# A rotated, quantised feed-forward stage on one core: three engines issue in a written order, and the butterflies run across two iterations

## The chip, the cores and the metric

The kernel runs on one core of a Trainium2 chip. A core has a matrix engine (TensorE, called PE in the profile, with its weight loads shown apart as PEld), a vector engine (VectorE, DVE), a scalar engine (ScalarE, ACT), a general engine (GpSimd, POOL) and a queue processor that issues transfers (SyncE, SP). Matrix products land in PSUM[...]. The metric is the time of one execution on the device in microseconds; it is given as the median of several runs, beside one execution that was profiled.

## The reference

The input is 128 sequences of 32 tokens with 512 features, 4096 rows in all. Three blocks follow each other, each with a layer norm in front and a residual add behind: a cross attention, a delta-rule attention with its own gated MLP, and a feed-forward block whose inputs are rotated by a Hadamard transform and rounded to 8 bits, with ternary weights. Only the last block concerns the change:

```python
def h_bitlinear(x, w):
    xq = act_quant(fwht(x))
    wq = weight_quant(w)
    return jnp.einsum('bsh,oh->bso', xq, wq)
gate = h_bitlinear(hidden_states, w_gate)
up = h_bitlinear(hidden_states, w_up)
return h_bitlinear(jax.nn.silu(gate) * up, w_down)
```

`fwht` is a Walsh-Hadamard transform over all features of a row (512 for gate and up, 2048 for down). `act_quant` takes the largest absolute value of a row, scales it to 127 and rounds.

## The kernel before, in words

The program is written in Python; each call becomes an instruction of one engine. A scheduler of the framework then orders the instructions of each engine by the place they have in the program and by its own estimate of when each can start, and it hands out buffers and adds the waits between engines. So the order in which an engine works need not be the order of the source.

The last block is the class `HadamardFfn`. Its loop in `run` (L1093) goes over 32 tiles of 128 rows, with work of several tiles in each pass, so that the engines overlap:

- Tile i+2 is turned: PE transposes its four 128-column blocks (`transposed`, L97), ACT copies them (L1016), PE multiplies each by a 128x128 Hadamard matrix (`rotated`, L917). The rest of the 512-point transform, the part across blocks, was done in the stage before. DVE takes the largest absolute value (L952), small DVE steps of one column make the scale `qs` from it (`scales`, L927, L929, L930), ACT multiplies by it and adds a large constant that rounds (`rounded`, L935, here called the lift), DVE subtracts the constant (L939), and SP issues a transfer that transposes the bf16 integers (L955).
- Tile i is multiplied by the gate and up weights in four pieces of 512 columns (`middle`, L1032). For each piece ACT computes Silu (L1036) and DVE the product (L1037). The result `m` has 2048 columns. DVE then does the part of the 2048-point transform that crosses blocks: `butterflies`, four rounds of an add and a subtract over half the tile each (L126, L127).
- Tile i-1's `m` is transposed on PE into four banks (L97) and copied by ACT (L1044), rotated into four banks (L917), reduced to the largest value by DVE (L1051, L1055), scaled, lifted by ACT (L935) and lowered by ACT (L937), and transposed by a transfer of SP (L1068).
- Tile i-3 is finished: 16 matmuls with the down weights (L1077), a scaling on ACT (L1082), an accumulating transfer on POOL that adds the residual (L1083), and the output transfer on SP (L1084).

All PSUM tiles of the stage come from one pool of eight banks. A tile of 128x512 f32 takes one bank, and a bank can be taken again when its reader is through. The last tile has a form of its own: its integers are transposed by PE, not by a transfer (L1066).

Two tiles go through the first bullet during the stage before (`first`). That stage, a gated MLP in f32, keeps PE full until the loop begins.

Of the kernel before, what the change touches and what calls it, by code (L numbers as in the profile page):

```python
# [897 lines left out]

class HadamardFfn:
# [7 lines left out]
    def __init__(self, g, x2, z2, mv2, had, ffn, out):  # L907
        self.g, self.tc, self.nc = g, g.tc, g.nc
        self.x2, self.z2, self.mv2, self.had, self.ffn, self.out = x2, z2, mv2, had, ffn, out
        self.right = dict(bufs=1, side="right", reuse_waits="tile")  # L910
        self.ready = {}

    def rotated(self, ps, xT, c0):

        pr = ps.tile([P, D], FP, name="ps")
        for c in range(DC):
            self.nc.tensor.matmul(  # L917
# [4 lines left out]
    def scales(self, st, mx, c):  # L922


        nc = self.nc
        m = st.tile([P, 1], FP, name="m")
        nc.vector.tensor_scalar(m, mx, c, Q_EPS, ALU.mult, ALU.max)  # L927
        qs = st.tile([P, 1], FP, name="qs")
        nc.vector.reciprocal(qs, m)  # L929
        nc.vector.tensor_scalar(qs, qs, c, 127.0, ALU.mult, ALU.mult)  # L930
        return m, qs

    def rounded(self, q, t, pr, qs, scalar):
        nc = self.nc
        nc.scalar.activation(t, pr, AF.Identity, bias=self.magic, scale=qs)  # L935
        if scalar:
            nc.scalar.activation(q, t, AF.Identity, bias=self.minus)  # L937
        else:
            nc.vector.tensor_scalar(q, t, MAGIC, None, ALU.subtract)  # L939

    def statistics(self, ns):

        nc, rstd = self.nc, self.rstd
        nc.scalar.activation(rstd[:, ns], self.mv2[:, ns, 1], AF.Sqrt, bias=self.g.ln_eps)
        nc.vector.reciprocal(rstd[:, ns], rstd[:, ns])
        nc.vector.tensor_scalar_mul(rstd[:, ns], rstd[:, ns], self.C1)

    def integers(self, i, pr, st, q, qT, t):

        nc = self.nc  # L950
        mx = st.tile([P, 1], FP, name="mx")
        nc.vector.tensor_reduce(mx, pr, AX.X, ALU.max, apply_absolute_value=True)  # L952
        m, qs = self.scales(st, mx, self.rstd[:, i : i + 1])
        self.rounded(q, t, pr, qs, False)
        nc.sync.dma_start_transpose(qT, q)  # L955
        f = st.tile([P, 2], FP, name="f")
        nc.vector.tensor_scalar_mul(f, self.both, m)
        self.ready[i] = qT, f

    def open(self, ctx):  # L960
# [14 lines left out]
        self.both = wp.tile([P, 2], FP, name="both")  # L975
        nc.vector.tensor_copy(self.both[:, 0:1], sg)
        nc.vector.tensor_copy(self.both[:, 1:2], su)
        self.rstd = wp.tile([P, NT // P], FP, name="rstd")

    def first(self, ps):  # L980
# [3 lines left out]
        for i in range(2):  # L984
# [4 lines left out]
            nc.scalar.copy(zT, self.g.transposed(ps, z, self.g.ident))  # L989
# [3 lines left out]
            self.integers(i, self.rotated(ps, zT, 0), wp, q, qT, z)  # L993
            yield 1

    def run(self):
        tc, nc, g, NG = self.tc, self.nc, self.g, self.NG
        wg, wu, rotated = self.wg, self.wu, self.rotated
# [4 lines left out]
        stack, (st, xp, wk1, wk, mp1, ps) = pools(  # L1003
            tc, ("d_st", 6), ("d_x", 4), ("d_wk1", 3), ("d_wk", 3), ("d_m1", 2), ("d_ps", 8, PSUM),
        )
        with mpool as mp, tc.tile_pool(name="d_w2", **self.right) as wp2, stack:
            wd = wp2.tile([P, IC, D], BF, name="wq2")
            z = {}
# [4 lines left out]

            def turned(i):
                zT = wk1.tile([P, DC, P], FP, name="zT")
                nc.scalar.copy(zT, g.transposed(ps, z.pop(i), g.ident))  # L1016
                return zT

            def integers(i, pr):
                q = wk1.tile([P, D], BF, name="q")  # L1020
                qT = wk1.tile([P, DC, P], BF, name="qT")
                self.integers(i, pr, st, q, qT, wk.tile([P, D], FP, name="t"))

            def middle(qT, f):

                m = mp.tile([P, IF], FP, name="m")
                for k in range(NG):
                    ks = slice(k * D, (k + 1) * D)
                    pg, pu = (ps.tile([P, D], FP, name="ps") for _ in range(2))
# [213 lines left out]
```

## Time and profile before

| what | value |
|---|---|
| median of 3 runs | 3041.19 us (3034.57 to 3048.02) |
| profiled execution, its own time | 3032.95 us |
| span from its first to its last instruction | 3031.2 us |
| PE busy over the span | 2896.5 us (96%) |
| DVE busy | 2002.5 us (66%) |
| ACT busy | 1055.8 us (35%) |
| first and last transposes of a zt tile (start of the loop's passes 0 and 29) | 2409.59 and 2941.02 us |
| last rotation of an m tile | 2990.13 us |

In a profile, a row of instructions has its start or its count, its busy time and what it wrote and read by the names of the program's tiles (`ps<-ident,m` is a transpose of m into a PSUM tile). Square brackets give how long the engine stood idle before the row, and which instruction ended that idle time. In the list of waits, the columns are the total in microseconds, how often, and the longest. A matmul's end is modelled and consecutive ones overlap, so the distance between starts is a better measure of PE than its busy time.

### The profile page before, as it was taken

To read this page: it belongs to the slowest core of one execution; us is meant where nothing else is said; L and a number is where in the kernel's file an instruction comes from. 1 tells how busy PE (TensorE), PEld (TensorE's weight loads), DVE (VectorE), ACT (ScalarE), POOL (GpSimd) and SP (SyncE) were. 2 spreads that over 40 slices of the span, in tenths; PEclk is the share of its full clock that TensorE was granted. 3 is DMA by queue.
4 is the path that set the end of the run, shared out by engine and by line. 5 is a ranking of instruction groups with operands and counts; after the bars stand their busy time and mean duration, and the time that the engine had idled before them with its cause. 6 is when DMAs were issued, how large, how long until landed. Compare 5 with 4: busy or idle time off the path is not lost.

```text
span 3031.2 us, 40875 instructions
## 1 busy us (share of the span) xinstructions
PE 2896.5 (96%) x14934; PEld 1647.3 (54%) x14934; DVE 2002.5 (66%) x3373; ACT 1055.8 (35%) x1779; POOL 659.2 (22%) x962
## 2 busy tenths in 40 slices
PE   8999999999999999599999999999999999999997
PEld 3444444443333333266766677676666766666664
DVE  2353444326699797368787877878522398888886
ACT  1111111205656666422111122111211256566564
POOL 1121212112686676221211110111100000000000
PEclk9999999999999999799999999999999999999999
DMA  9797998863554543742414132231411124443333
GB/s 327 265 312 268 330 310 305 289 223 93 170 149 124 175 136 109 209 139 62 132 58 126 53 123 77 79 100 42 132 49 46 65 56 77 77 78 78 75 73 62
DMA packets 342169, 428.47 MB, mean 141 GB/s; under 512 B 150225, under 2 KB 252753, under 8 KB 338513
## 3 DMA queue, kind: packets, MB, share of 16 engines
q1 hardware_dynamic: 305888, 325.93, 36.0%
q0 software_dynamic: 36080, 99.92, 10.9%
q8 instruction: 119, 1.95, 0.3%
q14 instruction: 82, 0.66, 0.1%
HBM read 288.36 MB, written 93.85 MB: 126 GB/s over the span
## 4 chain that ended last, share of the span: by engine, by line
PE 48%; DVE 10%; ACT 5%; issue 2%; DMA 1%; POOL 0%; SPq 0%; ACTq 0%; DVEq 0%; POOLq 0%
PE pm L823 9%; PE pm L826 9%; PE pm L834 9%; PE pp L520 5%; PE ps L797 4%; ACT t L935 2%; PE ps L917 2%; PE ps L1077 2%; ACT q L937 2%; PE ps L1032 2%; PE ps L764 2%; PE pg L455 2%; DVE mb L126 2%; PE ps L97 2%; DVE mx L1051 1%
## 5 line engine op out<-in xcount | busy, mean ns | idle before, releaser
L823 PE MATMUL pm<-hT,wg 128*128 128x256 f32 x1408 | 342.5, 386 | 0.2 <-ACT hT L812 0.2
L826 PE MATMUL pm<-hT,wu 128*128 128x256 f32 x1408 | 333.6, 380 | 0.0
L436 DVE TENSOR_TENSOR pr<-L,W 128x1984 f32<-128x1984 f32 (+30 forms) x248 | 313.0, 1262 | 23.7 <-DMA L<-ld 19.8
L442 DVE TENSOR_TENSOR W<-W,pr 128x1984 f32<-128x1984 f32 (+30 forms) x248 | 308.2, 1243 | 3.2
L834 PE MATMUL pm<-wd,mT 128*128 128x512 f32 x704 | 307.4, 592 | 0.0
L823 PEld LDWEIGHTS pm<-hT,wg 128*128 128x128 f32 x1408 | 262.4, 191 | 56.8 <-issue 16.2
L826 PEld LDWEIGHTS pm<-hT,wu 128*128 128x128 f32 x1408 | 267.8, 190 | 36.2
L834 PEld LDWEIGHTS pm<-wd,mT 128*128 128x128 f32 x704 | 132.5, 190 | 160.1 <-issue 159.9
L1032 PE MATMUL ps<-wq,qT 128*128 128x512 bf16 x960 | 218.7, 379 | 0.3
L828 ACT ACTIVATE sg<-pm 128x256 f32<-128x256 f32 x176 | 67.2, 382 | 345.9 <-PE pm L823 334.4
L829 DVE TENSOR_TENSOR mT<-pm,sg 128x256 f32<-128x256 f32 x176 | 73.7, 419 | 160.8 <-PE pm L826 146.1
L1083 POOL DMA_DIRECT2D xo<-x x31 | 26.3, 848 | 582.6 <-ACT xo L1082 526.2
L1032 PEld LDWEIGHTS <-qT 128*128 128x128 bf16 x960 | 93.7, 98 | 103.0 <-issue 4.6
L461 POOL TENSOR_TENSOR kk<-kk,cm 128x256 f32<-128x256 f32 x128 | 132.0, 1031 | 2.1
L458 POOL DMA_DIRECT2D ld<-kk x128 | 92.5, 722 | 151.6 <-ACT kk L457 144.5
L935 ACT ACTIVATE t<-ps,magic,qs 128x512 f32<-128x512 f32 x158 | 115.9, 777 | 19.5 <-DVE qs L930 19.3
L455 PE MATMUL pg<-kqm,kq 128*32 128x512 f32 x896 | 118.8, 601 | 3.5 <-DMA kqm<-kq 2.9
L917 PEld LDWEIGHTS ps<-hd,mT 128*128 128x128 f32 x1024 | 119.6, 192 | 4.3
L346 PE MATMUL ps<-hT,wq 128*128 128x512 f32 x256 | 114.4, 606 | 7.8 <-ACT hT L339 7.8
L1077 PE MATMUL ps<-wq,q2T 128*128 128x512 bf16 x512 | 120.6, 391 | 0.5 <-ACT t L935 0.3
L917 PE MATMUL ps<-hd,mT 128*128 128x128 f32 x1024 | 119.7, 275 | 0.0
L520 PE MATMUL pp<-hT,wk 128*128 128x512 f32 x256 | 117.6, 600 | 0.7 <-DVE acc L527 0.4
(224 smaller groups left out, 4939.9 us busy)
## 6 DMA issues: line engine op xcount, KB each, us to landing
kall<-in_ctxT_dram SPq DMA_DIRECT2D x32, 2056.0 KB
cx<-in_ctx_dram SPq DMA_DIRECT2D x32, 2048.0 KB
x<-xo POOLq DMA_DIRECT2D x64, 256.0 KB, 3.5
ld<-kk POOLq DMA_DIRECT2D x128, 128.0 KB, 2.6
pd<-kk POOLq DMA_DIRECT2D x128, 128.0 KB, 2.3
L<-ld SPq DMA_DIRECT2D x8, 2048.0 KB
pe<-pd SPq DMA_DIRECT2D x256, 64.0 KB
kqm<-kq SPq DMA_DIRECT2D x448, 32.0 KB
```

Source lines behind the costliest of these rows:

```text
L436: nc.vector.tensor_mul(pr[:, 0:n], bc(L[:, s, :, s + 1 : T].rearrange("p h t -> p t h"), HD), w[:, s].unsqueeze(1).to_broadcast([P, n, H4, ...
L442: nc.vector.tensor_sub(w[:, s + 1 :], w[:, s + 1 :], pr[:, 0:n])
L455: nc.tensor.matmul(pg[js], k[:, js], m[:, :, :, js], start=True, stop=True)
L461: nc.gpsimd.tensor_mul(kk[:, 1], kk[:, 1], cm.unsqueeze(1).to_broadcast([P, HH, T]))
L520: nc.tensor.matmul(pp.rearrange("p b t -> p (b t)"), w[n][:, dc, ec * P : (ec + 1) * P], hT[:, dc, :], start=dc == 0, stop=dc == DC - 1,)
L823: nc.tensor.matmul(pg, wg[:, dc, fs], hT[:, dc, :], start=dc == 0, stop=dc == DC - 1)
L826: nc.tensor.matmul(pu, wu[:, dc, fs], hT[:, dc, :], start=dc == 0, stop=dc == DC - 1)
L834: nc.tensor.matmul(pd, mT[:, fc, i * P : (i + 1) * P], wd[:, fc, :], start=fc == 0, stop=fc == FC - 1,)
L917: self.nc.tensor.matmul(pr[:, c * P : (c + 1) * P], xT[:, c0 + c, :], self.hd, start=True, stop=True)
L935: nc.scalar.activation(t, pr, AF.Identity, bias=self.magic, scale=qs)
L1032: nc.tensor.matmul(p, qT[:, dc, :], w[:, dc, ks], start=dc == 0, stop=dc == DC - 1)
L1077: nc.tensor.matmul(pd, qT[:, c, :], wd[:, c, :], start=c == 0, stop=c == IC - 1)
```

## The change

A new class `InOrder` wraps an engine; each instruction issued through it gets an edge to the previous one. The edge carries no semaphore; it only keeps the scheduler from exchanging the two. `run` wraps PE, ACT and DVE, and the loop is written anew so that the source has the order wanted on each of them. SP and POOL stay with the scheduler.

In a pass, the order is now as follows. PE: transposes of tile i+2, first gate/up piece, rotation of tile i+2, three gate/up pieces, transposes of m of tile i-1, down product of tile i-3, rotation of m of tile i-1. ACT: copy of tile i+2, first lift of tile i-2's second rounding, first Silu, three more lifts, two Silu, the first lowering, the fourth Silu, the lift of tile i+2, four copies of m, three lowerings, the scaling of tile i-3. DVE: the sixth butterfly of tile i-1, first product, the seventh and eighth, second product, the largest value and scales of tile i+2, third and fourth product, the lowering of tile i+2, four butterflies of tile i, the first reduction of tile i-1, the fifth butterfly of tile i, three reductions and the scale steps of tile i-1. The eight butterflies of a tile are a generator, of which five run in one pass and three in the next.

The second rounding of a tile thus begins in one pass and ends in the next, and its down product comes one pass after the integers instead of two. The transposed and the rotated z share a PSUM pool of one bank (`pz`); the other pool has seven. The lifts get a pool of six `t` tiles. The layer norm's factor of a row is moved out of the scale and into the constants `both` and `floor`, computed once for all tiles, so that `scales` has a multiplication and a reciprocal and no third step. After the loop the last two down products follow one after the other, the final tile being lowered by DVE alone.

```diff
+class InOrder:
+
+
+    def __init__(self, tc, engine):
+        self.tc, self.engine, self.last = tc, engine, None
+
+    def __getattr__(self, name):
+        method = getattr(self.engine, name)
+
+        def issue(*args, **kw):
+            ins = method(*args, **kw).ins
+            if self.last is not None:
+                self.tc.add_manual_dep(
+                    ins, self.last.name,
+                    mybir.DependencyInfo(
+                        mybir.DependencyClass.NoSync, mybir.DependencyReason.DATA
+                    ),
+                    reason="in order",
+                )
+            self.last = ins
+
+        return issue
...
-    def scales(self, st, mx, c):
-
-
-        nc = self.nc
+    def scales(self, st, mx, floor):
+
         m = st.tile([P, 1], FP, name="m")
-        nc.vector.tensor_scalar(m, mx, c, Q_EPS, ALU.mult, ALU.max)
+        self.dve.tensor_scalar(m, mx, floor, 1.0 / 127.0, ALU.max, ALU.mult)
         qs = st.tile([P, 1], FP, name="qs")
-        nc.vector.reciprocal(qs, m)
-        nc.vector.tensor_scalar(qs, qs, c, 127.0, ALU.mult, ALU.mult)
+        self.dve.reciprocal(qs, m)
         return m, qs
 
-    def rounded(self, q, t, pr, qs, scalar):
-        nc = self.nc
-        nc.scalar.activation(t, pr, AF.Identity, bias=self.magic, scale=qs)
-        if scalar:
-            nc.scalar.activation(q, t, AF.Identity, bias=self.minus)
-        else:
-            nc.vector.tensor_scalar(q, t, MAGIC, None, ALU.subtract)
+    def lifted(self, t, pr, qs):
+
+        self.act.activation(t, pr, AF.Identity, bias=self.magic, scale=qs)
...
+    def largest(self, i, pr, st):
+
         mx = st.tile([P, 1], FP, name="mx")
-        nc.vector.tensor_reduce(mx, pr, AX.X, ALU.max, apply_absolute_value=True)
-        m, qs = self.scales(st, mx, self.rstd[:, i : i + 1])
-        self.rounded(q, t, pr, qs, False)
-        nc.sync.dma_start_transpose(qT, q)
+        self.dve.tensor_reduce(mx, pr, AX.X, ALU.max, apply_absolute_value=True)
+        m, qs = self.scales(st, mx, self.floor[:, i : i + 1])
         f = st.tile([P, 2], FP, name="f")
-        nc.vector.tensor_scalar_mul(f, self.both, m)
+        self.dve.tensor_scalar_mul(f, self.both[:, i, :], m)
+        return qs, f
+
+    def integers(self, i, pr, f, qs, q, qT, t):
+
+        self.lifted(t, pr, qs)
+        self.dve.tensor_scalar(q, t, MAGIC, None, ALU.subtract)
+        self.nc.sync.dma_start_transpose(qT, q)
         self.ready[i] = qT, f
...
+            pr = self.rotated(ps, zT, 0)
+            qs, f = self.largest(i, pr, wp)
+            f0 = wp.tile([P, 2], FP, name=f"f{i}")
+            nc.vector.tensor_copy(f0, f)
+            self.integers(i, pr, f0, qs, q, qT, z)
             yield 1
...
+        pe, act, dve = (InOrder(tc, e) for e in (nc.tensor, nc.scalar, nc.vector))
+        self.pe, self.act, self.dve = pe, act, dve
...
-        stack, (st, xp, wk1, wk, mp1, ps) = pools(
-            tc, ("d_st", 6), ("d_x", 4), ("d_wk1", 3), ("d_wk", 3), ("d_m1", 2), ("d_ps", 8, PSUM),
+        stack, (st, xp, wk1, wk, tp, mp1, ps, pz) = pools(
+            tc, ("d_st", 6), ("d_x", 4), ("d_wk1", 3), ("d_wk", 3), ("d_t", 6), ("d_m1", 2),
+            ("d_ps", 7, PSUM), ("d_pz", 1, PSUM),
         )
...
+            def butterflies(i):
+
+                a, b = m[i], mp.tile([P, IF], FP, name="mb")
+                step = 1
+                while step < IC:
+                    x, y = (
+                        v.rearrange("p (a c d) -> p a c d", c=2, d=step * P) for v in (a, b)
+                    )
+                    dve.tensor_add(y[:, :, 0, :], x[:, :, 0, :], x[:, :, 1, :])
+                    yield
+                    dve.tensor_sub(y[:, :, 1, :], x[:, :, 0, :], x[:, :, 1, :])
+                    yield
+                    a, b, step = b, a, 2 * step
...
+            def last_rotated(mT, steps):
+
+
+                mx = st.tile([P, NG], FP, name="mx4")
+                pr = []
                 for k in range(NG):
-                    pt = g.transposed(ps, m[:, k * D : (k + 1) * D], g.ident)
-                    nc.scalar.copy(mT[:, k * DC : (k + 1) * DC, :], pt)
-                return mT
-
-            def last_integers(pr, end):
-
-                mx = st.tile([P, NG], FP, name="mx4")
-                for k in range(NG):
-                    nc.vector.tensor_reduce(
+                    pr.append(self.rotated(ps, mT, k * DC))
+                    dve.tensor_reduce(
                         mx[:, k : k + 1], pr[k], AX.X, ALU.max, apply_absolute_value=True
                     )
+                    if k == 0:
+                        go(steps, 1)
...
+                dve.tensor_reduce(mx1, mx, AX.X, ALU.max)
+                mm, qs = self.scales(st, mx1, Q_EPS / self.C2)
                 f = st.tile([P, 1], FP, name="fd")
-                nc.vector.tensor_mul(f, mm, sd)
-                return qT, f
+                dve.tensor_mul(f, mm, sdl)
+                return pr, qs, f
 
...
-            m, done = {}, {}
-            for i in range(n + 3):
-                if i + 2 < n:
-                    zT = turned(i + 2)
+            steps, last = iter(()), None
+            for i in range(n + 1):
+                cur, ahead = i < n, i + 2 < n
+                if ahead:
+                    zT = wk1.tile([P, DC, P], FP, name="zT")
+                    act.copy(zT, self.transposed(pz, z.pop(i + 2), g.ident))
                 if 0 < i and i + 5 < n:
                     load(i + 5)
-                if i < n:
-                    steps = middle(*self.ready.pop(i))
-                    m[i] = next(steps)
                 if i == n // 2:
                     self.statistics(slice(late, n))
-                if i + 2 < n:
-                    integers(i + 2, rotated(ps, zT, 0))
-                if i < n:
-                    for _ in steps:
-                        pass
-                if 0 <= i - 1 < n:
-                    mT = middle_turned(m.pop(i - 1))
-                if 0 <= i - 3:
-                    finish(i - 3, *done.pop(i - 3))
-                if i == n - 1:
-                    x_end = xp.tile([P, D], FP, name="zt")
-                    nc.sync.dma_start(x_end, self.x2[i * P :, :])
-                if 0 <= i - 1 < n:
-                    pr = [rotated(ps, mT, k * DC) for k in range(NG)]
-                    done[i - 1] = last_integers(pr, i == n)
-                if i < n:
-                    m[i] = butterflies(nc, m[i], mp.tile([P, IF], FP, name="mb"))
+                if cur:
+                    qT, f = self.ready.pop(i)
+                    m[i] = mp.tile([P, IF], FP, name="m")
+                    p = gate_up(qT, 0)
+                elif 0 <= i - 3:
+                    finish(i - 3, *qT2.pop(i - 3))
+                if last:
+                    pr2, qs2, f2 = last
+                    q2 = mp1.tile([P, IF], BF, name="q2")
+                    q2T = mp1.tile([P, IC, P], BF, name="q2T")
+                    t2 = [tp.tile([P, D], FP, name="t") for _ in range(NG)]
+
+                    def lowered(k):
+                        act.activation(
+                            q2[:, k * D : (k + 1) * D], t2[k], AF.Identity, bias=self.minus
+                        )
+
+                    self.lifted(t2[0], pr2[0], qs2)
+                go(steps, 1)
+                if cur:
+                    s = gated(p[0], f)
+                if last:
+                    for k in range(1, NG):
+                        self.lifted(t2[k], pr2[k], qs2)
+                if cur:
+                    times_up(m[i], 0, p[1], f, s)
+                go(steps, IC)
+                if ahead:
+                    pr = self.rotated(pz, zT, 0)
+                if cur:
+                    p = gate_up(qT, 1)
+                    times_up(m[i], 1, p[1], f, gated(p[0], f))
+                if ahead:
+                    qs, fn = self.largest(i + 2, pr, st)
+                if cur:
+                    p = gate_up(qT, 2)
+                    s = gated(p[0], f)
+                if last:
+                    lowered(0)
+                if cur:
+                    times_up(m[i], 2, p[1], f, s)
+                    p = gate_up(qT, 3)
+                    times_up(m[i], 3, p[1], f, gated(p[0], f))
+                if ahead:
+                    self.integers(
+                        i + 2, pr, fn, qs, wk1.tile([P, D], BF, name="q"),
+                        wk1.tile([P, DC, P], BF, name="qT"), tp.tile([P, D], FP, name="t"),
+                    )
+                if 0 <= i - 1:
+                    mT = turned(i - 1)
+                if last:
+                    for k in range(1, NG):
+                        lowered(k)
+                    nc.sync.dma_start_transpose(q2T, q2)
+                    qT2[i - 2] = q2T, f2
+                if cur and 0 <= i - 3:
+                    finish(i - 3, *qT2.pop(i - 3))
+                if cur:
+                    steps = butterflies(i)
+                    go(steps, NG)
+                if 0 <= i - 1:
+                    last = last_rotated(mT, steps)
+
+            x_end = xp.tile([P, D], FP, name="zt")
+            nc.sync.dma_start(x_end, self.x2[(n - 1) * P :, :])
+            finish(n - 2, *qT2.pop(n - 2))
+            pr, qs, f = last
+            q2T = mp1.tile([P, IC, P], BF, name="q2T")
+            q2 = mp1.tile([P, IF], BF, name="q2")
+            for k in range(NG):
+                t = tp.tile([P, D], FP, name="t")
+                self.lifted(t, pr[k], qs)
+                q = q2[:, k * D : (k + 1) * D]
+                dve.tensor_scalar(q, t, MAGIC, None, ALU.subtract)
+                copy = act.copy if k % 2 else dve.tensor_copy
+                copy(q2T[:, k * DC : (k + 1) * DC, :], self.transposed(ps, q, g.identb, BF))
+            finish(n - 1, q2T, f)
 
 
 @with_exitstack
```

## The prediction

> **What bounds the kernel now.** I read the page's first two parts, then the stretches, the waits and the timeline of the last stage.
>
> ```profile
> span 3031.2 us, 40875 instructions
> PE   8999999999999999599999999999999999999997
> PEclk9999999999999999799999999999999999999999
> ```
>
> ```profile
> 2650.00:2700.00 50.00, 47.49 (x294) 31.12 (x293) 42.47 (x71) 31.85 (x54) 2.54 (x3) 1.00 0.42 77
> ```
>
> The second block is a 50 us stretch of the stage that changes; its columns are PE, PEld, DVE, ACT and POOL busy (instructions in brackets), clock, DMA share, GB/s. The stage fills the last 620 us. PE is at 95% there, so it looks like the bound; but DVE (85%) is close, and a busy matmul row can hide a pause shorter than its modelled end. The pauses are clearer in the waits from 2472.9 to 2941, exactly 25 iterations:
>
> ```profile
> DVE q L939 <- ACT t L935: 50.5, 17, 3.0
> PEld ps L97 <- ACT t L935: 29.0, 49, 1.5
> ACT t L935 <- DVE qs L930: 13.7, 16, 1.1
> PEld ps L97 <- ACT s L1036: 5.5, 8, 0.7
> PEld ps L97 <- DVE m L1037: 3.6, 16, 0.3
> ```
>
> The weight loads of the transposes (L97) wait 29.0+5.5+3.6 = 38.1 us, 1.52 us an iteration, for a PSUM bank, mostly until ACT's first rounding step (L935) has read it. One iteration shows why the bank is late:
>
> ```profile
> 2658.37 2.48 DVE L1051 TENSOR_REDUCE mx<-ps 128x1 f32<-128x512 f32 x4
> 2659.89 0.60 PE L97 MATMUL ps<-ident,zt 128*128 128x128 f32 x4
> 2661.90 0.15 DVE L1055 TENSOR_REDUCE mx<-mx 128x1 f32<-128x4 f32 x1
> ...
> 2663.10 0.15 DVE L927 TENSOR_SCALAR m<-mx 128x1 f32<-128x1 f32 x1
> ...
> 2663.82 0.15 DVE L929 RECIPROCAL qs<-m 128x1 f32<-128x1 f32 x1
> ...
> 2665.08 0.15 DVE L930 TENSOR_SCALAR qs<-qs 128x1 f32<-128x1 f32 x1
> ...
> 2668.71 0.42 PEld L97 LDWEIGHTS ps<-ident,m 128*128 128x128 f32 x4 [0.92 <-ACT t L935]
> ...
> 2671.17 0.42 PEld L97 LDWEIGHTS ps<-ident,m 128*128 128x128 f32 x4 [0.69 <-ACT s L1036]
> ...
> 2671.84 3.61 PE L1077 MATMUL ps<-wq,q2T 128*128 128x512 bf16 x16
> ...
> 2675.29 3.73 PE L917 MATMUL ps<-hd,mT 128*128 128x128 f32 x32
> ```
>
> The reductions end at 2660.85; the scale that frees four banks is ready at 2665.23, because each 0.15 us step queues behind a 1.22 us butterfly. Starts of the zt transposes are 17.50, 18.98 and 19.42 us apart in rotation; over i=4 to 28 the mean is (2941.02−2472.95)/25 = 18.72.
>
> [...] two of the 25 iterations took 21.0 instead of 19.4, and their 50 us stretches show clock 0.97 against 1.00 above.
>
> **The change, part by part.** *PE floor.* PE executes the same instructions. Start to start in the timeline: zt transposes 0.43 (2659.89 to 2660.32), first gate/up half 1.73, rotation of z 0.89, 24 gate/up matmuls 5.2 (a row of 24 lasts 5.34, less its last one's overlap), 16 transposes of m 1.74 (0.109 each, the pitch in the row of four zt transposes), down 2671.84 to 2675.29 = 3.45, rotation of m 2675.29 to 2678.86 = 3.57. Sum 17.0; with hand-offs 17.1. That agrees with 18.63 (the three-step mean) less 1.52.
>
> *DVE, in the new order.* Pitches are start to start in the timeline. Eight butterflies at 1.14 (2663.95 to 2665.08), 9.12, plus 0.10 where the third reads the second (2674.33 to 2675.58 is 1.25); four gate products at 0.66, 2.64; five reductions at 0.60 (four last 2.48), 3.0; q 0.38. The small steps now follow each other directly, so each waits for the last: after the last reduction 0.12+0.19+0.19+0.08+0.12 = 0.70, as the tail already shows from 3010.38 to 3010.96; for z 0.12+0.25+0.08+0.11 = 0.56, as from 2413.73 to 2415.02. Sum 16.5. The two removed L930 would have cost about 0.2. The first gate product waits some 0.3 for ACT: 16.8. ACT: four Silu of 0.69, five lifts of 0.78, four lowerings of 0.72, copies 2.06+0.58, a scaling of 0.71: 12.9. PE remains the bound, with only 0.3 of cover on DVE.
>
> *The order laid side by side* (us after an iteration's start). The last rotation ends at 17.2 of the previous one, so its last scale is ready at about 1.7. ACT: zT 0.6, first lift 1.8 to 2.6, Silu to 3.2, three lifts to 5.2. DVE: sixth butterfly from 1.8, gate product 3.2, seventh and eighth to 6.2. PE needs m only at 8.3: cover 2.1. Lifts release banks at 2.6, 3.9, 4.5 and 5.2; taken in turn, PE wants them at 3.9, 4.8, 5.6 and 6.5: cover 1.1 to 1.4. Gate products end by 9.3, q 9.7, four butterflies 14.2; the first last-rotation bank is full at 14.6, so DVE is there first. If a cover is gone, the excess goes one to one on PE. I take 17.15 an iteration (17.0 to 17.5).
>
> *The bank for z, and eight minus one.* z's transposes and its rotation share a bank; its round trip ends when ACT lifts it at 8.9, before the next z at 17.1. Cost zero, behind 8 us; seven other banks are the cover counted above.
>
> *Transposing transfers.* SP still issues q2T, q's, the output and the z load. The down product follows q2T one iteration sooner: lowered by 12.9, wanted 10.1 into the next, 14.2 us later. No view gives that transfer's time. In the tail it starts issuing at 3006.03 and its user runs at 3016.30: at most 10.3; its packets end about 5 us after issue, so I take 5 (nothing exposed). An output queued on SP ahead would add about 6 and still fit.
>
> *Start.* Iteration 3 ended at 2472.95, 63.4 after 2409.59. In the new order DVE starts four butterflies at 9.4, then needs about 16.5 an iteration; PE waits for it in iterations 1 to 3 (banks not lifted) and ends iteration 3 at 62.1. Gain 1.3, bounds −4 and +5.
>
> *Middle.* i=4 to 31 took from 2472.95 to 2993.7 (last rotation's start 2990.13 + 3.57), 520.8. After: 28 x 17.15 = 480.2, less 2.7 for z's PE work absent from two = 477.5. Gain 43.3. This includes the two slow-clock iterations.
>
> *Tail.* From 2993.7 to the end, 37.5. PE no longer pauses 5.3 us for butterflies, but the last-but-one down product now stands ahead of the final transposes, and its ACT scaling ahead of the final lifts. Final rotation ends at 13; q2T of that tile, lowered at 12.7, is taken at about 18; the down product and scaling end at 22.5; four lift/lower/transpose/copy rounds of about 2 each end at 30.4; down to 33.4, final add and output to about 40. Loss 2.8, bounds −4 (a gain) and +6.
>
> *Once only.* Extra multiplies in the statistics, the f0 copies and moved scale constants are under ten small DVE operations; zero, beside the last mlp block's PE work. The second statistics call may put two ACT_TABLE_LOAD of 1.28 in mid-stage: at most 2.6, behind ACT's 4.2 spare.
>
> Sum 1.3+43.3−2.8 = 41.8: the profiled execution, 3032.95, becomes 2991.2. The runs' median is 8.2 above that execution; taking that offset along, 2999.
>
> **Rivals.** (A) As above: 2982 to 3012; floor 17.0, better ends and the spread of 13 us among the runs give the lower end. (B) DVE becomes the bound: 0.3 us of cover is little, and every wait in a fixed DVE order is paid. Before, DVE stood idle 2.4 us an iteration, but could fill in with ready work. For it: 16.8 against 17.1. Against it: those idles were mostly q behind ACT (50.5/25), which now follows an ACT queue that is early. At 17.9: 28x0.75 = 21 more, 3020. (C) The gain is not there: the same banks stay late (the lifts now wait for reductions at the iteration's boundary, ahead of Silu), and the start loses what the middle gains. At 18.6, 3040. Against it: the scale chain shrinks from 4.4 us after its reductions to about 1. (D) Slower: the down product, first of a strict queue, waits for q2T. It decides from 14.2+2 = 16.2 us after the last lowering, since 2 us an iteration (28x2 = 56) eats the gain; at 17 us, 2999+28x2.8 = 3077. For it: SP must wait for an accumulating write before each output. Against it: 5 us seen.
>
> **How the numbers follow.** A change of 0.5%, 15 us, is what can be told from none. Chances A 0.65, B 0.16, C 0.10, D 0.09; A and B are faster (0.81), C the same, D slower. The range holds A and B with the run spread: 2980 to 3028; the likeliest case alone is 2982 to 3012.
>
> **What would show it.** Right: zt starts 17.0 to 17.5 apart; no weight load of L97's successor waiting for a lift; the scale within 1.5 us of the last reduction; DVE near 95%; no 0.97 clock in the middle. B: PE waits on DVE's eighth butterfly or on lifts late for qs, DVE without idle time. C: zt starts above 18.4. D: PE idle ahead of the down product, ended by a DMA. Wrong would be a DVE sum off by 5%, banks assigned otherwise than in turn, or a tail longer than 46.

## The result and the profile after

The changed kernel takes 2992.93 us in the median of six runs (2982.3 to 2995.91), the kernel before 3035.48 (six runs, 3030.14 to 3048.02). The ratio is 0.985, with an interval of [0.983, 0.987]: 1.5% faster. The forecast was 2999, in a range of 2980 to 3028. The profiled execution of after took 2991.72 us; its span is 2989.9.

The stage of the change, cut at the same places in both traces (us). It begins with the first transposes of a zt tile; the middle runs from those of pass 4 to the end of the rotation of m in pass 31 (its start and 3.57); the tail is what follows:

| | before | after | after by the prediction |
|---|---|---|---|
| start, passes 0 to 3 | 63.36 | 62.57 | 62.1 |
| middle, passes 4 to 31 | 520.75 | 473.58 | 477.5 |
| tail | 37.48 | 38.80 | 40.3 |
| whole stage | 621.59 | 574.95 | 579.9 |
| all that lies before the stage | 2409.59 | 2414.99 | 2409.59 |

The stage gained 46.6 us, 4.8 more than predicted. In this profiled execution the work before the stage took 5.4 us longer, of which some 3.4 by an estimate (half of 6.8): stretches of half clock (granted 0.50) between 1227 and 1296 us, in another stage, add up to 47.8 us there and to 41.0 before. The rest was not traced to a cause. In the nine traces of the changed kernel and of kernels made from it, the stage begins between 2406.2 and 2417.8 us, so 5.4 us lies within the spread of executions. So the profiled execution's 2991.72 falls on the sum's 2991.2 by luck: 4.8 too little gain and 5.4 of something else.

From the page of after, its span, PE's tenths and the granted clock:

```profile
span 2989.9 us, 40853 instructions
...
PE   8999999999999999699999999999999999999997
...
PEclk9999999999999999799999999999999999999999
```

The tenths look as before, since 95% and 100% both print a 9. The stretch from 2650 to 2700 us shows the difference (columns: PE, PEld, DVE, ACT, POOL busy with counts, clock, DMA share, GB/s):

```profile
2650.00:2700.00 50.00, 50.00 (x321) 33.97 (x320) 48.03 (x73) 34.47 (x57) 2.54 (x3) 1.00 0.42 87
```

PE is busy throughout, with 321 matmul records where before had 294 in the same 50 us. DVE rose from 85% to 96%. The waits from 2472 to 2910 us follow; after issues everything of the loop through one helper, so all lines read L909 and the tiles tell what it is:

```profile
ACT t L909 <- DVE qs L909: 16.7, 28, 1.6
...
DVE m L909 <- ACT s L909: 6.1, 26, 0.2
DVE mx L909 <- PE ps L909: 5.0, 22, 0.2
```

No row of PE or PEld is left; before, weight loads for the transposes of m (L97) waited 38.1 us in passes 4 to 28. One pass, which begins at 2664.62 with the transposes of zt:

```profile
2663.88 1.88 DVE L909 TENSOR_REDUCE mx<-ps 128x1 f32<-128x512 f32 x3
2664.62 0.60 PE L909 MATMUL ps<-ident,zt 128*128 128x128 f32 x4
...
2665.79 0.16 DVE L909 TENSOR_REDUCE mx<-mx 128x1 f32<-128x4 f32 x1
...
2666.17 0.16 DVE L909 RECIPROCAL qs<-m 128x1 f32<-128x1 f32 x1
...
2666.37 0.78 ACT L909 ACTIVATE t<-ps,magic,qs 128x512 f32<-128x512 f32 x1 [0.53 <-DVE qs L909]
...
2667.62 2.12 ACT L909 ACTIVATE t<-ps,magic,qs 128x512 f32<-128x512 f32 x3
...
2672.78 0.77 ACT L909 ACTIVATE t<-ps,magic,qs 128x512 f32<-128x512 f32 x1
2672.85 1.91 PE L909 MATMUL ps<-ident,m 128*128 128x128 f32 x16
```

The scale stands within 0.6 us of the last reduction instead of 4.4, the lifts follow, and the 16 transposes of m form one row with no wait in it. The next zt transposes come 17.00 later; every pass from 2477.56 on takes 17.00 to 17.01.

### The profile page after: what moved, and what is told of

It reads as the page before. It is cut to its first block, busy times and chain, and to the rows that moved or that the text cites. A ratio compares the mean times of both kernels' runs of the same rounds, so it can differ in the third digit from the quotient of the medians.

```text
span 2989.9 us, 40853 instructions
## 1 busy us (share of the span) xinstructions
PE 2879.6 (96%) x14934; PEld 1649.2 (55%) x14934; DVE 2008.9 (67%) x3318; ACT 1057.1 (35%) x1777; POOL 659.4 (22%) x962
## 4 chain that ended last, share of the span: by engine, by line
PE 59%; DVE 5%; DMA 2%; issue 1%; ACT 1%; SPq 0%; POOL 0%; DVEq 0%; ACTq 0%; POOLq 0%
PE ps L909 17%; PE pm L823 9%; PE pm L834 9%; PE pm L826 9%; PE pp L520 5%; PE ps L797 4%; PE pg L455 2%; PE ps L764 2%; DVE W L442 1%; DVE pr L436 1%; DMA xs<-x 1%; PE ps L97 1%; DMA wd<-in_WdownT_dram 1%; DVE m L909 0%; PE pm L455 0%
## 5 line engine op out<-in xcount | busy, mean ns | idle before, releaser
L823 PEld LDWEIGHTS pm<-hT,wg 128*128 128x128 f32 x1408 | 262.1, 191 | 57.0 <-issue 16.2
L909 PE MATMUL ps<-wq,qT 128*128 128x512 bf16 x960 | 217.1, 379 | 3.0 <-ACT t L909 3.0
L909 DVE TENSOR_TENSOR mb<-m 128x1024 f32<-128x1024 f32 x128 | 153.1, 1217 | 0.1
L909 DVE TENSOR_TENSOR m<-mb 128x1024 f32<-128x1024 f32 x128 | 150.7, 1219 | 1.2
L909 PEld LDWEIGHTS <-qT 128*128 128x128 bf16 x960 | 93.9, 98 | 103.7 <-issue 3.9
L909 ACT ACTIVATE t<-ps,magic,qs 128x512 f32<-128x512 f32 x158 | 115.7, 781 | 37.7 <-DVE qs L909 37.7
L909 PEld LDWEIGHTS ps<-hd,mT 128*128 128x128 f32 x1024 | 120.7, 194 | 8.9 <-ACT mT L909 4.8
L909 PE MATMUL ps<-hd,mT 128*128 128x128 f32 x1024 | 121.4, 278 | 4.1 <-ACT mT L909 4.1
L909 PE MATMUL ps<-wq,q2T 128*128 128x512 bf16 x512 | 120.2, 389 | 3.8 <-DMA q2T<-q 3.8
```

What stands on the lines that cost most here:

```text
L823: nc.tensor.matmul(pg, wg[:, dc, fs], hT[:, dc, :], start=dc == 0, stop=dc == DC - 1)
L909: ins = method(*args, **kw).ins
```

## Experiments

Four questions: does the held order pay, what else does, how much cover has DVE, and what does the tail's order cost. In the tables and texts, "middle" and "tail" are cut as above.

### Is it the order?

**The chain off.** The changed source, without the edges, so that the scheduler may exchange neighbours.

```diff
-        pe, act, dve = (InOrder(tc, e) for e in (nc.tensor, nc.scalar, nc.vector))
+        pe, act, dve = nc.tensor, nc.scalar, nc.vector
```

> The changed kernel without the chain: the same source order, split butterflies and banks, but the scheduler may again exchange instructions of PE, ACT and DVE. My theory (what pays is that the order is held, above all the scale steps standing directly behind the last reduction): the steps fall between butterflies again, PE's transposes of m wait for banks, passes 18 to 19 us apart, 28 x 1.0 to 2.0 = 28 to 55 us lost, so 3020 to 3045. Rival (the new source order, the split and the shorter scale do it, and the chain changes little): passes 17.0 to 17.3, 2990 to 3003.

Measured: 2991.95 us, ratio 0.985 [0.983, 0.987], the same as the changed kernel. The passes take 17.03, later 17.21; the middle is 6.5 us longer than with the edges (480.06), the tail 3.3 shorter (35.46). The theory that the held order earns the gain fell: the edges are worth 0.23 us a pass, and in the sum nothing. Its timeline (L1121 and L960 are small steps of the scale, L1090 is a butterfly, L965 the lifts):

```profile
2684.76 0.15 DVE L1121 TENSOR_REDUCE mx<-mx 128x1 f32<-128x4 f32 x1
2684.87 1.23 DVE L1090 TENSOR_TENSOR m<-mb 128x1024 f32<-128x1024 f32 x1
...
2686.74 0.15 DVE L960 RECIPROCAL qs<-m 128x1 f32<-128x1 f32 x1
...
2686.92 2.78 ACT L965 ACTIVATE t<-ps,magic,qs 128x512 f32<-128x512 f32 x4 [0.23 <-DVE qs L960]
```

The small steps still stand between long DVE work, and the lifts come 5.0 us into the pass instead of 1.75, yet PE hardly waits. So the late scale, in which the prediction saw the reason for the late banks, can't be all of it.

**The butterflies unsplit.** All eight before the reductions of the same pass, with the edges; then the same source without them.

```diff
-                    go(steps, NG)
+                    go(steps, IC)
```

> The changed kernel with all eight butterflies of a tile ahead of the reductions of its own pass, none carried over. My theory: DVE's sum is the same 16.5 a pass, but the first product now directly follows the scale steps and waits for lift and Silu (about 0.1+0.66+0.69 = 1.45 us, which the sixth butterfly filled), and the scale comes some 4 us later in the pass, so passes of 17.6 to 18.2 with DVE as the bound: 28 x 0.6 to 1.2 = 17 to 34 more than 2993, so 3010 to 3027. Rival (the split is only cosmetic, since DVE has 4% idle time and PE leads): 17.0, 2993.

Measured: 3091.18 us, ratio 1.018 [1.016, 1.020]: slower than before. Most passes take 18.95 and 21.68 by turns, some 19.99 each; the mean is 20.24 where 17.6 to 18.2 was expected. One of the long ones, which began at 2889.05:

```profile
2892.04 2.47 DVE L909 TENSOR_REDUCE mx<-ps 128x1 f32<-128x512 f32 x4
...
2895.12 0.78 ACT L909 ACTIVATE t<-ps,magic,qs 128x512 f32<-128x512 f32 x1 [4.85 <-DVE qs L909]
2895.80 0.68 ACT L909 ACTIVATE s<-ps,f 128x512 f32<-128x512 f32 x1
2895.95 4.64 PE L909 MATMUL ps<-wq,qT 128*128 128x512 bf16 x13 [2.82 <-ACT t L909]
...
2896.51 0.75 DVE L909 SCALAR_TENSOR_TENSOR m<-ps,f,s 128x512 f32<-128x512 f32 x1 [1.37 <-ACT s L909]
...
2899.09 0.75 DVE L909 SCALAR_TENSOR_TENSOR m<-ps,f,s 128x512 f32<-128x512 f32 x1 [1.83 <-ACT s L909]
```

One late thing crosses three queues. The reductions begin 3 us into the pass and the first lift follows them. PE, which has no bank for its next gate/up piece, waits for this lift (2.82). The first Silu stands behind the lift in ACT's fixed order, and DVE's product waits for that Silu (1.37). The second Silu then stands behind three lifts, until 2898.36, and DVE waits again (1.83). After PE's pause the granted clock is 0.53 over 3.60 us (the same columns as above):

```profile
2897.00:2900.60 3.60, 3.60 (x10) 1.27 (x9) 1.73 (x4) 3.25 (x6) 0.00 (x0) 0.53 0.00 0
```

The other half of the pair:

> The changed kernel with all eight butterflies of a tile issued ahead of the reductions of its pass, as in the run that took passes of 20.2, but without the edges between neighbours, so that the scheduler may exchange them. If the scheduler repairs an order that is bad on DVE (it may take reductions or scale steps between butterflies once their input is there by its own estimate): passes of 17.2 to 18.4, total 2992 to 3030. If it keeps the source's order: 19.5 to 20.5 a pass, total 3070 to 3095.

Measured: 3008.67 us (3005.3 to 3015.07), ratio 0.992 [0.990, 0.994]. Passes of 17.08, 18.36 and 18.24; the middle is 498.9. The scheduler repairs most of the bad order, 566.6 to 498.9, by taking reductions between butterflies. It doesn't reach the split source: against 480.06, the split is worth 18.8 us without edges, and 93 with them. What remains in this kernel goes with a scale that comes late in the pass, ready at 2694.70:

```profile
2692.41 2.79 PE L1066 MATMUL ps<-wq,qT 128*128 128x512 bf16 x12 [0.78 <-ACT s L1074]
...
2694.95 2.78 ACT L965 ACTIVATE t<-ps,magic,qs 128x512 f32<-128x512 f32 x4
```

The pass began at 2685.75: the lifts come 9.2 us in, and PE waits for a bank at 6.7. A Silu ends that wait. That PE runs short because four banks still wait for the lifts is an inference; no run tests it.

**The old source, chained.** The kernel before with edges in the order of its own source, on the three engines.

```diff
-        nc = self.nc
+        nc = self.nc = g.nc = Chained(tc, self.nc)
```

> The kernel before with its own source order, held by the same chain on PE, ACT and DVE in the loop. My theory (the chain pays only with the right order): its source puts all eight butterflies behind the scale of the tile before, so after PE's last rotation come reduction and scale 1.5, butterflies 9.2, then PE's transposes 1.7, down product 3.45 and rotation 3.57: a ring of 19.5 us, passes 19 to 20, slower than before by 28 x 0.5 to 1.4 = 14 to 40: 3050 to 3075. Rival (any held order beats the scheduler's, since scale steps then follow their reductions): 17.5 to 18.3, 3002 to 3025.

Measured: 3226.59 us, ratio 1.061 [1.060, 1.063]; passes of 24.4 to 25.8 where 19 to 20 was expected, with a mean clock of 0.961 (0.987 in before); in the pass below the rotation of z lasts 2.08 us, against 1.05 in the pass of the unsplit kernel. My estimate had missed ACT's queue. There the copy of zT stands behind four pairs of lift and lowering, from 2869.11 on, and PE can't rotate z without it:

```profile
2874.18 0.72 ACT L910 ACTIVATE q<-t,minus 128x512 bf16<-128x512 f32 x1
2874.81 0.56 ACT L910 COPY zT<-ps 128x512 f32<-128x512 f32 x1
...
2875.42 2.08 PE L910 MATMUL ps<-hd,zT 128*128 128x128 f32 x8 [5.74 <-ACT zT L910]
```

Edges thus earn nothing by themselves; with them the kernel keeps a good order and a bad one alike.

### What does pay?

**z in the common pool.** The changed kernel, with eight banks for all.

```diff
-            ("d_ps", 7, PSUM), ("d_pz", 1, PSUM),
+            ("d_ps", 8, PSUM),
...
-                    act.copy(zT, self.transposed(pz, z.pop(i + 2), g.ident))
+                    act.copy(zT, self.transposed(ps, z.pop(i + 2), g.ident))
...
-                    pr = self.rotated(pz, zT, 0)
+                    pr = self.rotated(ps, zT, 0)
```

> The changed kernel with z's transposes and rotation taken from one pool of eight banks instead of a bank of their own. My theory: no part of the gain hangs on the separate bank; every bank was free 1.1 us or more before PE wanted it, passes stay at 17.0, 2988 to 2998. Rival (the own bank keeps z's slow round trip, 2.6 to 8.9 us into a pass, out of the rotation): PE waits for banks again, 0.3 us or more a pass, 3001 or more.

Measured: 2988.61 us, ratio 0.984 [0.982, 0.986]; passes of 17.01, the middle 473.48. In the written order the bank of its own for z is worth nothing.

**The shorter scale alone.** The kernel before, with layer norm's factor moved into the constants and no third step; the order left to the scheduler.

```diff
-        nc.vector.tensor_scalar(m, mx, c, Q_EPS, ALU.mult, ALU.max)
+        nc.vector.tensor_scalar(m, mx, c, 1.0 / 127.0, ALU.max, ALU.mult)
         qs = st.tile([P, 1], FP, name="qs")
         nc.vector.reciprocal(qs, m)
-        nc.vector.tensor_scalar(qs, qs, c, 127.0, ALU.mult, ALU.mult)
```

> The kernel before with only the shorter scale: the row factor moved into constants, so that the third one-column step is gone; the order stays with the scheduler. My theory: a part of the gain is here even without a held order, since that step stood behind a whole butterfly: the banks come up to 1.2 us earlier in a pass, PE's wait of 1.5 falls to 0.5 to 1.2, passes 17.6 to 18.3, 9 to 28 us less than 3035: 3007 to 3026. Rival (the scheduler rearranges and the banks are as late as before): 3030 to 3040.

Measured: 3023.34 us (3017.53 to 3026.73), ratio 0.996 [0.995, 0.997]. The passes settle at 18.26 and the middle at 507.65: 13.1 us of the 47.2. The two passes of 21.0 in the middle of before are gone too.

**The lifts grouped.** The kernel before, with six `t` tiles and the four lifts ahead of the four lowerings; and the same together with the shorter scale.

```diff
+                t = [tp.tile([P, D], FP, name="t") for _ in range(NG)]
+                if not end:
+                    for k in range(NG):
+                        nc.scalar.activation(t[k], pr[k], AF.Identity, bias=self.magic, scale=qs)
                 for k in range(NG):
                     ks = slice(k * D, (k + 1) * D)
-                    self.rounded(q[:, ks], wk.tile([P, D], FP, name="t"), pr[k], qs, scalar)
...
+                        nc.scalar.activation(q[:, ks], t[k], AF.Identity, bias=self.minus)
```

> The kernel before, order left to the scheduler, with one thing of the change: the t tiles have a pool of six, and the four lifts of a tile's second rounding are issued together, ahead of its four lowerings (before, lifts and lowerings go in pairs, two by two, because t has three buffers). The old long scale chain, between the butterflies, stays. Theory L (the banks come late because the lowerings, 0.7 us each, stand between the lifts): in the old order the third and fourth lift end 2.7 us later than they would without the two lowerings ahead of them, and PE waits 1.5 us a pass on lifts; so passes of 17.2 to 17.9 instead of 18.6, total 2998 to 3020. Rival S (it is the late scale that keeps the banks, or ACT's next Silu now waits behind four lifts): passes of 18.3 to 18.8, total 3025 to 3042.

> The kernel before with two things of the change together: the lifts grouped in a pool of six, and the shorter scale chain (layer norm's factor moved into constants). No written order, no split of the butterflies, no early down product, no bank for z. Theory L+S (these two free the banks early enough): passes of 17.0 to 17.4, total 2988 to 3003, within 0.3% of the changed kernel; the loop's other rewriting then earned nothing but its tail. Rival (the split of the butterflies, which puts the reductions ahead of them, is needed too): passes of 17.6 to 18.2, 18.25 being what the shorter scale reached alone; total 3008 to 3024.

Measured: the grouped lifts alone take 3042.4 us (3034.47 to 3048.29), ratio 1.003 [1.001, 1.004], the middle 525.5. Both together take 3024.24 (3016.91 to 3036.1), ratio 0.997 [0.996, 0.998], the middle 507.78, which is the shorter scale's 507.65. So theory L fell, and so did the theory that the two together free the banks early enough: with the four lifts together and 4.7 us into the pass, the passes take 18.26, as long as with the shorter scale alone. This is the kernel with both (L1079 are lowerings, L934 the lift of z, L1073 the four lifts of m):

```profile
2677.97 2.79 ACT L1073 ACTIVATE t<-ps,magic,qs 128x512 f32<-128x512 f32 x4
...
2680.63 2.56 ACT L1079 ACTIVATE q<-t,minus 128x512 bf16<-128x512 f32 x4
...
2683.08 0.78 ACT L934 ACTIVATE t<-ps,magic,qs 128x512 f32<-128x512 f32 x1
...
2683.91 0.42 PEld L97 LDWEIGHTS ps<-ident,m 128*128 128x128 f32 x4 [1.19 <-ACT t L934]
2683.91 0.66 PE L97 MATMUL ps<-ident,m 128*128 128x128 f32 x4 [0.95 <-ACT t L934]
```

The bank that PE lacks is z's. Its scale has been ready since 2681.84, but its lift stands behind four lowerings, which free no bank, and ends 10.6 us into the pass; the last four transposes of m want the bank at 9.5. Their weight loads wait 1.19 us, nearly the whole 1.25 by which these passes exceed 17.01. In the kernel with the shorter scale alone they wait 1.19 for the same lift. In the changed kernel only one lowering stands ahead of z's lift, which ends 8.93 us in; three lowerings come behind the copies.

The grouping alone is a little worse than before. In one pass of three PE's transposes wait 1.92 us for a lift of z that begins 11.0 us in. In before they wait 1.23 in one pass of three, for a lift of z that begins 11.0 in as well; PE comes to it later there, held up by lifts of m. Behind the wait of 1.92 that ends at 2691.52 lies a stretch of 3.41 us at half clock (0.50 from 2692.14 to 2695.55); in before, two of the waits of 1.23 have one behind them. The mean clock of the profiled execution is 0.981, of before's 0.987.

What each step brought, all without edges but the last row:

| kernel | middle | per pass (middle/28) | step |
|---|---|---|---|
| before | 520.75 | 18.60 | |
| shorter scale | 507.65 | 18.13 | −0.47 |
| and grouped lifts | 507.78 | 18.14 | 0.00 |
| rest of the new source, butterflies unsplit | 498.90 | 17.82 | −0.32 |
| butterflies split | 480.06 | 17.15 | −0.67 |
| edges (the changed kernel) | 473.58 | 16.91 | −0.23 |

The table is one path through the parts; others would share the gain out differently. Two things stay open, since they weren't tried: the kernel with the shorter scale and only the lift of z moved ahead of the lowerings, and the same with only a bank for z. In the free order z's lift ends 10.3 us into the pass even in the new source, so there the bank of its own may earn what it doesn't in the written order.

### How much cover has DVE?

Extra work that leaves the output as it is, in the changed kernel: a third one-column step in both scales; one addition on 512 columns a pass; one on 1024.

```diff
         self.dve.reciprocal(qs, m)
+        self.dve.tensor_scalar(qs, qs, 1.0, 1.0, ALU.mult, ALU.mult)
```

> The changed kernel with a third one-column step put back into both scale chains (a multiplication by one). My theory: two more DVE steps of about 0.2 us, each waiting for the one before; DVE's real cover is what it stands waiting for PE's first last-rotation bank, 0.23 us, so the pass goes to 17.0 to 17.25, at most 7 us in all. Rival (the shorter scale is itself a main part of the gain): 17.5 or more.

```diff
+                    dve.tensor_add(pad, pad, pad)
```

> The changed kernel with one more add of 128x512 f32 on DVE in each pass (0.6 us), on a tile nobody reads. If DVE's cover is only its 0.23 us of waiting for PE, the pass becomes 17.3 to 17.45 and the time 28 x 0.3 to 0.45 = 8 to 13 more. If the 4% that DVE is idle (0.66 us a pass) is all free, the pass stays at 17.0.

> The same with 128x1024 (1.14 us). Cover of 0.23: passes of 17.85 to 18.0, some 25 more. Cover of 0.66: 17.5, some 13 more. If PE were the only bound with cover to spare: 17.0.

Measured, one execution each: 2998.25, 3000.65 and 3013.37 us. The step leaves passes of 17.00 to 17.01 until about the 20th, then 17.08; with the cover below that makes 0.39 for both steps, where the prediction had 0.2. The additions, 0.60 and 1.14 us from their start to the next instruction's, give 17.29 and 17.83: 0.28 and 0.82 more than 17.01, so 0.32 of each is hidden. That is the cover, not the 4% of idle time that the stretch shows (0.67 us a pass); the rest hid nothing of work put in at this place, such as the 0.23 a pass in which the first product waits for Silu (6.1 us in 26 passes). Beyond 0.32, the added work costs one to one.

### The tail

**Another order at the end.** The changed kernel; in the loop's last pass, which multiplies no new tile, ACT lifts before it scales tile n-3. After the loop the final four lifts are issued together, and the final tile's transposes go ahead of the last-but-one down product.

```diff
-            finish(n - 2, *qT2.pop(n - 2))
             pr, qs, f = last
...
+            t = [tp.tile([P, D], FP, name="t") for _ in range(NG)]
+            for k in range(NG):
+                self.lifted(t[k], pr[k], qs)
             for k in range(NG):
-                t = tp.tile([P, D], FP, name="t")
-                self.lifted(t, pr[k], qs)
...
+            finish(n - 2, *qT2.pop(n - 2))
             finish(n - 1, q2T, f)
```

> The changed kernel with another order after the last full pass only: ACT's lifts come ahead of the scaling of the tile before, the final tile's lifts are issued together and its transposes stand ahead of the last-but-one down product. My theory: in the changed kernel PE waits 3.8 us for the last-but-one transposed integers with the final transposes queued behind, and the final lifts wait 8.4 us behind that tile's scaling; both go, the stretch from the last full pass to the end falls from 38.8 to 27 to 31 us, 8 to 12 us less than 2993: 2981 to 2985. Rival (the final chain of add, rounding and output transfer is what the end waits for, in any order): less than 3 us.

Measured: 2981.75 us (2980.41 to 2984.67), ratio 0.982 [0.980, 0.984]; the tail is 31.72 instead of 38.80. That is 7.1 us less, where 8 to 12 was expected; the medians differ by 11.2. The profiled executions differ by 10.0, and the 2.9 beyond the tail lie before the stage, where this order changes nothing. It is the fastest of all kernels here. In the changed kernel's tail PE and ACT stand still for a transfer:

```profile
2967.03 5.31 PE L909 MATMUL ps<-wq,q2T 128*128 128x512 bf16 x16 [3.78 <-DMA q2T<-q]
2972.38 0.69 ACT L909 ACTIVATE xo<-ps,fd 128x512 f32<-128x512 f32 x1 [9.72 <-PE ps L909]
2972.96 1.44 ACT L909 ACTIVATE t<-ps,magic,qs 128x512 f32<-128x512 f32 x2
```

That transfer was issued at 2962.68. The final scale is there at 2964.56, but the lifts begin at 2972.96, behind the scaling of a product that waits for q2T. With the other order the lifts begin at 2959.76, 0.09 us after the scale, and both down products run in one row:

```profile
2959.76 2.79 ACT L909 ACTIVATE t<-ps,magic,qs 128x512 f32<-128x512 f32 x4 [1.88 <-DVE fd L909]
...
2964.59 9.20 PE L909 MATMUL ps<-wq,q2T 128*128 128x512 bf16 x32
```

## Why the prediction was right, and where not

**PE floor: right.** 17.0 start to start was summed from single rows; the passes take 17.01. I took 17.15 to be safe. The middle's 28 times 0.14 are the 3.9 us by which 477.5 missed 473.58; the 2.7 for z's work absent from two passes fits to 0.1.

**DVE's sum and cover: right.** Predicted 16.8 of 17.1, with 0.3 of cover; the pads measured 0.32. They put DVE's own round at 16.69 (17.29 less 0.60, and 17.83 less 1.14) against PE's 17.01, so both terms were 0.1 too high and the difference fits better than they do. Rival B was thus as near as stated, and didn't come about.

**The order side by side: right.** After the start of the pass, predicted against the pass shown: scale at 1.7, 1.71; lifts of m done at 5.2, 5.12; eighth butterfly 6.2, 6.16; q 9.7, 9.63; four butterflies 14.2, 14.29; first bank of the last rotation full 14.6, reduced from 14.52; lowering done 12.9, 12.75. That the written order is the one that runs was assumed; in the trace of after PE's 108, ACT's 19 and DVE's 25 instructions of a pass come in that order in passes 4 to 28 without exception.

**A bank for z at no cost: right** in the written order, as the pool of eight shows.

**The transposing transfer: right.** I took 5 us after the issue; in the tail the down product could start 4.35 after the issue began. Rival D needed 16.2. It showed only in the tail, where nothing lies between the lowering and the product: 3.78 us of wait.

**Start and tail: right in sign.** Gain 0.8 for 1.3, loss 1.3 for 2.8. In the start PE waits largely as forecast: in pass 1 for a butterfly (1.27) and a copy of m (1.90), in passes 2 and 3 for lifts (0.68 and 2.30). For the tail I named the wait behind the down product and its scaling, which the other order took away.

**The offset: wrong.** I added the 8.2 us by which the runs' median stood above the profiled execution. That distance came from three runs; with six it is 2.5, and for after it is 1.2. This is why 2999 is 6 too high, the sum itself having met 2991.72 by luck.

**Why the banks were late: wrong in part.** The step that failed reads "mostly until ACT's first rounding step (L935) has read it", followed by the scale that queues behind butterflies. L935 is two kinds of lift, of m and of z, and I laid the whole wait on the late scale of m. Sorted one by one over passes 4 to 28 of before, the 29.0 us that weight loads of transposes wait for L935 are some 17.3 for lifts of m (41 waits) and 11.8 for z's (8 waits). In the pass that the prediction shows, both waits for a lift (0.92 and one of 0.25) are for m. Two passes earlier the long one is for z:

```profile
2630.62 0.42 PEld L97 LDWEIGHTS ps<-ident,m 128*128 128x128 f32 x4 [0.47 <-ACT t L935]
2631.29 0.42 PEld L97 LDWEIGHTS ps<-ident,m 128*128 128x128 f32 x4 [0.25 <-ACT t L935]
2633.18 0.42 PEld L97 LDWEIGHTS ps<-ident,m 128*128 128x128 f32 x4 [1.47 <-ACT t L935]
```

The last wait ends with z's lift, which began at 2632.35 and stood behind lowerings on ACT. With the shorter scale the waits for m fell from 17.3 to 5.0 us, but those for z rose from 11.8 to 29.8, now in all 25 passes; with the grouped lifts too they are 0 and 29.9. So the late lifts of m were the larger part of the wait, as forecast, but taking it away let the other take its place, and the shorter scale alone brought 0.47 of the 1.69 us a pass. The sum was spared, since it was made from the order after and not from the waits taken away.

Three small readings were off too, and change little. Of the four small steps of m's scale, three stand behind a butterfly and the reciprocal behind a gate product. DVE's idle time before is 2.6 us a pass, not 2.4. The packets of the tail's transposing transfer ended 3.8 us after its issue began, not 5.

**What the edges are worth: not priced, and then misjudged.** The prediction treated order and edges as one. My first theory, that holding the order earns the gain, fell with the first experiment. In the expectations the two bad orders were then undersized by 2 to 6 us a pass: one late instruction crosses from queue to queue, and half clock comes on top (mean clock 0.979 and 0.961, against 0.985 in the changed kernel).

## What to carry to other kernels

Forecast a software pipeline from its new order: floor of the bound engine, sum of the next one, and each buffer's release against the time it is wanted; that gave the time of a pass to 0.14 us, while the story of the old waits was half wrong. Ask of each wait which instance of the line it is for, and what PE would wait for next if it were gone. In an engine's queue, what frees a scarce buffer is better ahead of what frees nothing; here that is argued from the waits, since no run moved z's lift alone. An order written by hand is safe only where all engines' queues are laid side by side: the same edges held passes of 17.0 and of 25.

## What the runs showed of the hardware

Stretches of half clock (granted 0.50) last 3.41, 6.83 or 10.24 us in the last stage of the traces of before and after, where the end of the kernel doesn't cut them. The two in the middle of before begin 225.28 us apart, at 2633.59 and 2858.87; that is 66 times 3.413, a third of 10.24. PE had paused ahead of the stretches looked at: 1.23 us in before, 1.92 in the kernel with grouped lifts and 2.82 in the unsplit one.

The length of a pause doesn't decide alone. In passes 4 to 28 of before PE pauses for 1.23 us eight times, and two of these pauses were followed by a stretch. Sum PE's idle time there in steps of 3.413 us, counted from the start of a stretch, as far as the profile's modelled ends show it: the step just ahead of each of the two holds 1.47 us, and no other more than 1.23. Two cases in one trace make no rule; what sets these pauses apart was not shown.

The two passes of before with such a stretch took 21.03 and 21.05 us instead of 19.42. Half of 3.41 is 1.7, near the 1.6 that they took longer; so a pause on PE like these may cost some 1.7 us beyond itself (an estimate from these numbers).
